# A planned instruction order made anew, with token maxima read from SBUF, in a kernel of soft mixture-of-experts, attention and gated layers

## The chip, the cores and the metric

The kernel runs on one core of one Trainium2 chip. The core has five engines with a queue each, worked off in order: PE (TensorE, the matrix multiplier), DVE (VectorE), ACT (ScalarE), POOL (GpSimd) and SP (SyncE, which here only issues DMAs). PE writes its results into PSUM; DVE and ACT read them there; POOL works on SBUF alone. The metric is the device time in microseconds of one execution, lower being better: the median of several runs. Everything is computed in float32.

## The reference, cut to what matters

The input `x` has 8 batches of 256 tokens of 128 features. Two groups of layers follow each other, and each sublayer adds to `x`:

```python
# soft mixture of experts: 16 experts of 64 slots, used in both groups
x1 = layernorm(x); se = layernorm(slot_embeds) * scale
logits   = einsum('bnd,esd->bnes', x1, se)
dispatch = softmax(logits, axis=1)                      # over the 256 tokens
combine  = softmax(logits.reshape(b, n, -1), axis=-1)   # over the 1024 slots
slots = einsum('bnd,bnes->besd', x1, dispatch)
eout  = (gelu(slots @ Wg + bg) * (slots @ Wu + bu)) @ Wd + bd
out   = einsum('bns,bso->bno', combine, eout)
# linear attention: elu + 1 features, 16 heads
# gated unit: gelu(gelu(silu(h w1) * (h w2) @ h1) @ h2) @ w3, ternary weights with scales
# random-feature attention (exp of projections, 16 heads of 32 features)
```

Each softmax needs maxima of the logits: `dispatch` one for each slot (over tokens), `combine` one for each token (over slots).

## The kernel before

**Steps and a planner.** The kernel doesn't issue its instructions where the Python text stands. Each piece of work is a *step* (`step`, L88): the engines that may do it with a planned length in ns each, the function that issues it, and the cells that it reads, writes and takes. `Plan.place` (L121) is a list scheduler. It takes the engines' clocks from 0 and repeatedly chooses among the steps that are ready the one that can start earliest (`rank = (at, s.key + 4 * late, s.number)`); a step's time `at` is the largest of its readiness (the end of what it needs, plus `LAG` of that engine), of its engine's free time, and of the time at which buffers of the kinds in `kinds` come free. Ties go to the smaller key. A key is the sum of planned PE time of the steps before it in the text, plus a shift of the step's part: the list `SHIFTS` (L16) has one number for each `plan.part()`, times 100. `TABLE` is the time for a change of ScalarE's function table. `Plan.issue` then writes the instructions in order of planned start. The plan is made when the kernel is built; on the chip each engine works through its queue in that order and waits on semaphores where it must.

**Lengths.** `act`, `dve`, `mms` and `flips` (L344 to L353) give planned lengths from a number of columns; other steps have a number written out.

**Norms.** `normalized` (L376) does a list of tiles of 128 x 128: per tile `bn_stats` and `bn_aggr` on DVE (L389, L390), then for all of them the *root* on POOL (L396 adds epsilon, L397 negates the mean, L398 raises to the power -0.5), then per tile one subtract and multiply (L404) on POOL or DVE, whichever the plan chooses. `norm` calls it for the two tiles of one batch.

**Dispatch of one batch** (`dispatch`, L547). The normalised tiles are flipped by PE (L359), copied with gain and bias by `affinely` (L446 on ACT, L448 on DVE), and spilled to DRAM and spread back in another layout by SP (L532, L539). Then come four pairs of logits matmuls (L568), each into one PSUM bank; each bank is copied to `comb` in SBUF (`evacuated`, L366 on ACT or L368 on DVE), and from the second on `greater` (L585, DVE) folds it into the token maxima `pm`. Its operands are the bank in PSUM and `comb` or `pm` in SBUF. After that, per half: `greatest` (L602, slot maxima, DVE), `exps` (L610, ACT), `inverse` (L618, DVE), `divided` (L623, POOL), a 32 x 32 block transpose (L631, DVE). PE gathers the slots (L644), and `affinely` writes them to `slots`. Last come the token maxima: `fold` (L661, DVE), two flips on PE, `token_max` (L672, DVE), two flips that spread them, a copy to `mb`; per half `less` (L690, POOL, subtracts them from `comb`) and an exponential (L696, ACT).

**The rest.** `experts` (L702) does 16 experts for four batches: L737 on PE, gelu L743 on ACT, L748 on DVE, L768 on PE. `combine` uses the exponentials of `comb` on PE (L809). Linear attention, gated units (`glu`; hidden products L1027) and random-feature attention follow. `group` (L1331 and on) runs this for four batches; the second group's keys are 45000 behind the first's. Layer 0 of a group calls `dispatch` for its four batches, then `experts`, then `combine` and the linear attention; layer 1 dispatches again. `weights` (L493) makes the block form of the projection weights (L504, DVE) once; `keys` (L453) normalises and flips the slot embeddings, two tiles at a time, into `seT`. Before all that PE multiplies the identity 14 times (`rehearse`).

Of the kernel before, what the change touches and what calls it, by code (L numbers as in the profile page):

```python
# [16 lines left out]
    -8021, -27496, -1880, -1692, -1246, -501, -3204, 428, -619, -9733, -3313, -704, -1426, -388,  # L17
    -970, -129, -74, -103, -98, -154, -167, -106, -115, -156, 74, -10, 102, 250, -97, -196,
    -808, -874, -909, -1074, 29, -1029, 38, -111, -648, 535, -462, -23, -50, -46, -16, -1, 45,
    -562, 6, 33, 30, -14, -15, 47, -634, -353, -62, -19, -6, 44, -80, -305, -75, -37, 23, -70,  # L20
    -46, -140, -62, -95, -51, -7, 41, 139, 595, 203, 505, 395, 466, 392, -421, -1494, -1666,
    -2400, -2447, -1620, -1321, -147, -1647, -2470, -682, -344, -440, -906, -1682, 131, 665,
    -678, -83, -257, -81, -105, -245, 128, -452, -242, 175, -164, 141, 89, -2895, 491, 27, -9,
    -309, 123, -400, -112, -68, -126, -154, -4, 30, -1, -18, -53, -63, -43, 40, -109, 28, -904,
    -346, -1059, -568, -335, 16, 114, 82, -63, 7, -540, -76, -46, 99, 125, 392, 168, 417, 581,
    1301, 1493, 564, -700, -58, 34, -703, -2087, -162, -669, 52, -105, 30, 443, -275, -282, 125,
    71, -25, 243, -231, -44, -662, -1357, -653, 10, 151, 122, 159, 89, 55, 401, -644, -846,
    -602, 288, 144, 168, 196, -340, 177, 49, -830, 47, 184, 1167, 295, 347, 468, 213, -1051,
    -596,
# [34 lines left out]
class Plan:  # L64
# [7 lines left out]
    LAG = {"PE": 300, "ACT": 120, "DVE": 100, "POOL": 150, "SP": 2600}  # L72
    TABLE = 1300
# [14 lines left out]
    def step(self, engines, run, reads=(), writes=(), takes=(), table=None):  # L88
        s = Step(len(self.steps), engines, run, table, self.key + self.shift)
        s.part = self.parts  # L90
        for c in reads:
            if c in self.writer:
                s.needs.add(self.writer[c])
        for c in writes:
            if c in self.writer:
                s.needs.add(self.writer[c])
            s.needs.update(self.readers.get(c, ()))
        for c in reads:
            self.readers.setdefault(c, set()).add(s)
        for c in writes:  # L100
            self.writer[c] = s
            self.readers[c] = set()
        s.needs.discard(s)
        for c in (*reads, *writes, *takes):
            b = c[0] if isinstance(c, tuple) else c
            if isinstance(b, Buf) and b not in s.bufs:
                s.bufs.append(b)
                b.left += 1
        self.steps.append(s)
        if "PE" in engines:  # L110
            self.key += engines["PE"]
        return s

    def given(self, at, cells):

        s = Step(-1, {}, None, None, 0)
        s.end, s.engine = at, "SP"
        for c in cells:
            self.writer[c] = s

    def place(self):  # L121
# [6 lines left out]
        free = dict.fromkeys(names, 0)  # L128
# [5 lines left out]
        def enable(s):  # L134
            s.ready = max((n.end + self.LAG[n.engine] for n in s.needs), default=0)
# [6 lines left out]
        while len(order) < len(self.steps):  # L142
            best = None
            for e in names:
                for s in able[e]:
                    at = max(s.ready, free[e])
                    short = {}
# [22 lines left out]
            if s.table:  # L170
                table = s.table
            for b in s.bufs:
# [6 lines left out]
            for b in s.bufs:  # L179
                b.left -= 1  # L180
                b.last = max(getattr(b, "last", 0), s.end + self.LAG[e])
# [19 lines left out]
def macaron_kernel(ctx: ExitStack, tc: tile.TileContext, i: dict, out: bass.AP):  # L201
# [65 lines left out]
    def fetched(dst, src, reads, writes):  # L267
        step({"SP": 430}, lambda _: nc.sync.dma_start(dst(), src), reads, writes)

    def x_in(b, n):  # L270
        fetched(
            lambda: x[:, b * TT : (b + n) * TT], i["x"][:, b * TT : (b + n) * TT],
            [], [("x", b + k) for k in range(n)],
# [70 lines left out]
    def act(n, pointers=False):  # L344
        return 160 + 0.83 * n + 100 * pointers

    def dve(n, extra=0):
        return 150 + 1.05 * n + extra

    def mms(*columns):  # L350
        return sum(2 * max(112, 0.84 * n) for n in columns)

    def flips(n):  # L353
        return 110 * n
# [21 lines left out]
    def normalized(tiles, twice=False):  # L376
# [9 lines left out]
        def stats(_):  # L386
            for t, (_, src, _, _) in enumerate(tiles):
                st = mv.ap[:, 8 + 6 * t : 14 + 6 * t]
                nc.vector.bn_stats(st, src())  # L389
# [10 lines left out]
        step({"DVE": 455 * n}, stats, [t[2] for t in tiles], [mv], takes=[t[3] for t in tiles])  # L400
        step({"POOL": 780 + 160 * n}, root, [mv], [mv])
        for t, (dst, src, r, w) in enumerate(tiles):
# [6 lines left out]
            step({"POOL": 480, "DVE": 430}, apply, [r, mv], [w])  # L409

    def norm(b, twice=False, y=None, at=0):

        y = y or Buf("k1", (P, TT, D))
        normalized(
            [
                (lambda t=t: y.ap[:, at + t, :], lambda t=t: x[:, b * TT + t, :],
                 ("x", b), (y, at + t))
# [4 lines left out]
        return y  # L422
# [18 lines left out]
    def affinely(dst, src, r, w, n):  # L441
# [8 lines left out]
        step({"ACT": act(n, True) + 90, "DVE": dve(n, 120)}, run, [*r, "ng"], w)  # L450


    def keys():  # L453
# [8 lines left out]
        for h in range(4):  # L462
            js = range(2 * h, 2 * h + 2)
            normalized(
                [
                    (lambda j=j: se_n.ap[:, j, :], lambda j=j: se_raw.ap[:, j, :],
                     (se_raw, h), (se_n, j))
                    for j in js
                ]
            )  # L470
# [22 lines left out]
    def weights():  # L493
# [24 lines left out]
        step({"POOL": 1900}, scaled, ["w3T", "s3"], ["w3T", "s3"])  # L518
# [7 lines left out]
    def replicated(y, b):  # L526
# [14 lines left out]
        step({"SP": 1800}, spill, [(y, t) for t in range(TT)], [("y", b)])  # L541
        step({"SP": 1800}, spread, [("y", b)], [yr])
# [4 lines left out]
    def dispatch(b, sl):  # L547
# [4 lines left out]
        y = norm(b, True)  # L552
# [10 lines left out]
        for u in range(4):  # L563
            pl = ps_(2, N)

            def logits(_, u=u, pl=pl):
# [10 lines left out]
                takes=[(comb, u), pm],  # L577
# [5 lines left out]
            if u:  # L583
                def greater(_, u=u, pl=pl):
                    nc.vector.tensor_tensor(  # L585
                        pm.ap, pl.ap, comb.ap[:, 0:2, :] if u == 1 else pm.ap, ALU.max
                    )

                step({"DVE": dve(2 * N)}, greater, [pl, pm, (comb, 0)], [pm])
# [6 lines left out]
        for h in range(2):  # L596
# [9 lines left out]
            step({"DVE": dve(4 * N)}, greatest, half, [mx])  # L606
# [8 lines left out]
            step({"ACT": 2200}, exps, [*half, mx], [mx, (ex, h)], table="exp")  # L615
# [4 lines left out]
            step({"DVE": 200}, inverse, [mx], [mx])  # L620
# [7 lines left out]
            step({"POOL": 1950}, divided, [mx, (ex, h)], [(ex, h)])  # L628
# [7 lines left out]
            step({"DVE": 1200}, turn, [(ex, h)], [(ex, h)])  # L636
# [12 lines left out]
        step({"PE": 3600}, gathered, [yr, (ex, 0), (ex, 1)], pos)  # L649
# [9 lines left out]

        def fold(_):  # L660
            nc.vector.tensor_tensor(pm.ap[:, 0], pm.ap[:, 0], pm.ap[:, 1], ALU.max)  # L661

        step({"DVE": 790}, fold, [pm], [pm])
# [21 lines left out]
        for h in range(2):  # L685
# [12 lines left out]
            step({"POOL": 2400}, less, [mb, *half], half)  # L698
# [3 lines left out]
    def experts(sl):  # L702
# [10 lines left out]
        def fetch(e):  # L713
# [11 lines left out]
            step({"SP": 1900}, run, [(sl, "in", BG - 2, 0)], [we])  # L725
            return we

        def front(e, we):
            j, k = e // 2, e % 2
            ht = Buf("k2", (P, 2, BG * S))  # L730
            for c in range(2):
# [25 lines left out]
                step({"DVE": dve(256, 65)}, up, [pe, ga], [(ht, c)])  # L757
            return ht

        def back(j, wes, hts):  # L760
# [3 lines left out]
            def down(_):  # L764
# [10 lines left out]
                {"PE": mms(*[P] * 2 * BG)}, down,  # L775
# [14 lines left out]
            step({"POOL": 120}, twos, [], whole(j))  # L790
# [11 lines left out]
    def combine(b, comb, sl, eo):  # L802
# [26 lines left out]
        step({"DVE": 900}, add, [(po, t) for t in range(TT)] + [("x", b)], [("x", b)], takes=[rc])  # L829

    def plus_bias(b, bias):
# [4 lines left out]
        step({"POOL": 750}, run, [("x", b)], [("x", b)])  # L836
# [30 lines left out]
    def linear(b):  # L867
        plan.part()
        yt = transposed(norm(b), TT)
# [37 lines left out]
        step({"ACT": act(512)}, exps, [kq], [kq], table="exp")  # L907
        step({"DVE": dve(512, 65)}, elu, [pk, kq], [kq])
# [5 lines left out]
        step({"POOL": 110}, ones, [pv], [(v1, 1)])  # L914
# [23 lines left out]
        step({"DVE": 730}, blocks, [pkv], [kv])  # L938
# [18 lines left out]
        step({"DVE": 1000}, divided, [po], [oh], takes=[rd])  # L957
# [5 lines left out]
    def combined_weights(name, scales, bufs, b):  # L963
# [12 lines left out]
        step({"SP": 2500}, fetch, [("x", b)], [*bufs, s])  # L976
# [9 lines left out]
        step({"POOL": 4 * 1050}, scaled, [*bufs, s], bufs)  # L986
# [8 lines left out]
        step({"POOL": 4 * 1200}, sums, bufs, bufs)  # L995
# [4 lines left out]
    def hidden(h, to, t4, w, wbufs):  # L1000
# [9 lines left out]
        def sub(dst, a, b, r, w):  # L1010
# [5 lines left out]
            step({"POOL": 1450, "DVE": 950}, run, r, w)  # L1016
# [30 lines left out]
        def gelu(i, k, src, r):  # L1047
# [3 lines left out]
            step({"ACT": act(512)}, run, r, [(to, i, k)], table="gelu")  # L1051
# [26 lines left out]
    def glu(b, after):  # L1078
# [8 lines left out]
        for k in range(2):  # L1087
            norm(b + k, False, y, k * TT)
# [3 lines left out]
        for o in range(NO):  # L1092
# [22 lines left out]
            step({"DVE": dve(512, 65)}, product, [pu, si], [(h, o // 2, k) for k in range(2)])  # L1115
# [27 lines left out]
    def favor(b):  # L1143
        plan.part()
        yt = transposed(norm(b), TT)
# [28 lines left out]
        step({"POOL": 1050}, squares, [(qk, 0)], [(qk, 1)])  # L1174
# [17 lines left out]
        step({"PE": 240}, half_norms, [(qk, 1)], [ph], takes=[hn])  # L1192
# [21 lines left out]
        for c, pw in enumerate(pws):  # L1214
# [13 lines left out]
            step({"DVE": 1550}, shifted, [pw, pn], [(phi, k, c) for k in range(2)], takes=[mx])  # L1228
        for k in (1, 0):
# [5 lines left out]
            step({"ACT": act(1024)}, exps, cells, cells, table="exp")  # L1235
# [49 lines left out]
        def turn_sums(_):  # L1285
# [4 lines left out]
            {"PE": 920}, sums, [*((phi, 1, c) for c in range(4)), v1], [pk], takes=[kv, kvm]  # L1290
        )
        step({"DVE": 430}, blocks, [pk], [kvm])
# [32 lines left out]
        step({"PE": 900}, products, [(qk, 0), (qk, 1), kv], [po], takes=[ot, rd])  # L1325
        step({"ACT": act(N), "DVE": dve(N)}, guarded, [po], [rd])
        step({"DVE": 2200}, divided, [po, rd], [ot])
# [3 lines left out]
    def group(g):  # L1331
        bs_ = range(g * BG, (g + 1) * BG)
        for layer in range(2):
            sl = Buf("slots", (P, NJ, 2, BG, S1))
            combs = {b: dispatch(b, sl) for b in bs_}
# [10 lines left out]
        def store(b):  # L1346
# [3 lines left out]
            step({"SP": 500}, run, [("x", b)], [])  # L1350
# [16 lines left out]
    step({"PE": 6000}, rehearse, [], [pwarm])  # L1367
# [76 lines left out]
```

## Time and profile before

| what | value |
|---|---|
| time, median of 3 runs | 762.42 us (761.95 to 763.28) |
| the profiled execution, its own time | 763.33 us |
| its span from first to last instruction | 761.6 us |
| busy: PE, DVE, ACT, POOL | 744.1, 527.4, 436.3, 321.2 us |
| matmuls of L737 (experts) | 512, 120.7 us |
| matmuls of L1027 (gated units), both forms | 896, 207.8 us |
| L585, token maxima, both forms, DVE | 48, mean 674 and 672 ns |
| L661, their fold, DVE | 16, mean 1056 ns |
| L404 on DVE; on POOL | 37, mean 644 ns; 59, mean 477 ns |
| L690 and L623 on POOL | 32 each, mean 2370 and 1906 ns |
| mean DMA over the span | 60 GB/s |

A PE matmul of float32 is two instructions in the profile. PE's time is its matmuls' time, with modelled ends; weight loads (PEld) run beside it. In the 40 slices of the page each digit is a tenth of a slice of 19.04 us, and PEclk is the granted clock, so the 8 in the first two slices means that PE ran below its full clock for a part of them.

### The profile page before, as it was taken

The page shows a single profiled execution, that of the slowest core. Times are in us where ns is not written, and L with a number is a line of the kernel's source. Part 1 is how long each engine was busy: PE and PEld are TensorE (multiplying, and loading weights), DVE is VectorE, ACT ScalarE, POOL GpSimd, SP SyncE. Part 2 cuts the span into 40 slices and gives each one's busy share as a digit, 9 for nine tenths or more (in the row PEclk, how much of TensorE's full clock was granted, in tenths as well). Part 3 has the DMA queues.
Part 4 walks back from the last instruction along what each step waited for, and adds up shares of the span by engine and source line. Part 5 has one row for each costly group of instructions (what it writes and reads, how often), then busy time and mean ns, then how long its engine had stood idle before and what let it go on. Part 6 is the DMA issues. An engine that isn't in the chain of part 4 may idle for free.

```text
span 761.6 us, 15125 instructions
## 1 busy us (share of the span) xinstructions
PE 744.1 (98%) x5884; PEld 623.3 (82%) x5884; DVE 527.4 (69%) x1085; ACT 436.3 (57%) x806; POOL 321.2 (42%) x418
## 2 busy tenths in 40 slices
PE   7889999999999999999999999999999999999998
PEld 6667788999889988889788987778867878878787
DVE  5898987467988787889645357756496737775432
ACT  2876988365676566791834245645265555493432
POOL 7766653442266652548901064334151622223020
PEclk8899999999999999999999999999999999999999
DMA  4634443113451043516322100000000000000000
GB/s 119 175 102 110 119 134 97 46 49 109 128 170 44 2 115 96 153 54 195 91 92 76 42 1 1 2 1 0 1 1 2 1 1 1 1 15 15 1 1 28
DMA packets 29911, 45.53 MB, mean 60 GB/s; under 512 B 5008, under 2 KB 18704, under 8 KB 29840
## 3 DMA queue, kind: packets, MB, share of 16 engines
q1 hardware_dynamic: 29840, 44.57, 19.7%
q8 instruction: 46, 0.75, 0.4%
q14 instruction: 25, 0.20, 0.1%
HBM read 41.41 MB, written 3.15 MB: 59 GB/s over the span
## 4 chain that ended last, share of the span: by engine, by line
PE 92%; DVE 4%; POOL 1%; issue 1%; ACT 1%; DMA 0%; DVEq 0%; POOLq 0%; ACTq 0%
PE ps L1027 26%; PE ps L737 14%; PE ps L768 8%; PE ps L809 8%; PE ps L644 7%; PE ps L568 6%; PE ps L359 4%; PE ps L1127 4%; PE ps L1100 4%; PE ps L1097 4%; PE ps L1206 1%; PE ps L1272 1%; PE ps L1306 1%; PE ps L857 1%; DVE comb L631 1%
## 5 line engine op out<-in xcount | busy, mean ns | idle before, releaser
L737 PE MATMUL ps<-slots,we 128*128 128x256 f32 x512 | 120.7, 385 | 0.4 <-DVE k L748 0.4
L737 PEld LDWEIGHTS ps<-slots,we 128*128 128x128 f32 x512 | 95.4, 192 | 14.9 <-issue 2.3
L1027 PE MATMUL ps<-comb,slots 128*128 128x256 f32 x448 | 104.0, 380 | 0.0
L1027 PE MATMUL ps<-comb,comb 128*128 128x256 f32 x448 | 103.8, 381 | 0.0
L1027 PEld LDWEIGHTS ps<-comb,slots 128*128 128x128 f32 x448 | 83.7, 190 | 15.3 <-issue 4.2
L1027 PEld LDWEIGHTS ps<-comb,comb 128*128 128x128 f32 x448 | 83.4, 190 | 13.0 <-issue 2.4
L690 POOL TENSOR_TENSOR comb<-comb,k 128x1024 f32<-128x1024 f32 x32 | 75.3, 2370 | 42.8 <-ACT k L366 32.0
L623 POOL TENSOR_TENSOR comb<-comb,sm 128x1024 f32<-128x1024 f32 x32 | 60.8, 1906 | 66.1 <-DVE sm L618 66.0
L366 ACT COPY k<-ps 128x512 f32<-128x512 f32 (+2 forms) x67 | 33.5, 503 | 86.9 <-PE ps L1027 61.9
L743 ACT ACTIVATE k<-ps,small 128x256 f32<-128x256 f32 x128 | 57.4, 474 | 42.5 <-PE ps L737 40.4
L748 DVE SCALAR_TENSOR_TENSOR k<-ps,small,k 128x256 f32<-128x256 f32 x128 | 56.9, 475 | 22.7 <-ACT k L743 22.3
L644 PE MATMUL ps<-comb,k 32*128 32x256 f32 x1024 | 65.1, 393 | 3.2 <-issue 1.3
L610 ACT ACTIVATE comb<-comb,sm 128x256 f32<-128x256 f32 x128 | 63.2, 496 | 7.6 <-DVE sm L602 7.5
L568 PE MATMUL ps<-k,seT 128*128 128x256 f32 x256 | 63.5, 394 | 1.7 <-ACT k L446 0.9
L644 PEld LDWEIGHTS ps<-comb,k 32*128 32x128 f32 x1024 | 54.8, 192 | 10.4 <-issue 3.0
L1049 ACT ACTIVATE comb<-comb 128x512 f32<-128x512 f32 x48 | 29.9, 629 | 58.0 <-DVE comb L1041 57.8
L768 PEld LDWEIGHTS ps<-we,k 128*64 128x64 f32 x1024 | 55.3, 137 | 9.4 <-issue 5.0
L768 PE MATMUL ps<-we,k 128*64 128x128 f32 x1024 | 62.5, 276 | 0.0
L1041 DVE TENSOR_TENSOR comb<-ps,k 128x512 f32<-128x512 f32 x48 | 32.9, 687 | 40.7 <-PE ps L1027 31.4
L809 PE MATMUL ps<-slots,comb 128*128 128x129 f32 x512 | 60.0, 276 | 0.0
L809 PEld LDWEIGHTS ps<-slots,comb 128*128 128x128 f32 x512 | 58.6, 192 | 1.3 <-issue 1.2
L1012 POOL TENSOR_TENSOR comb<-comb 128x512 f32<-128x512 f32 x18 | 27.3, 1519 | 75.9 <-DVE comb L1106 47.5
(147 smaller groups left out, 1354.0 us busy)
## 6 DMA issues: line engine op xcount, KB each, us to landing
we<-in_We SPq DMA_DIRECT2D x64, 384.0 KB, 3.9
k<-y SPq DMA_DIRECT2D x64, 128.0 KB, 2.8
y<-k SPq DMA_DIRECT2D x64, 32.0 KB, 1.9
we<-in_bd SPq DMA_DIRECT2D x64, 32.0 KB, 3.6
comb<-in_h2T SPq DMA_DIRECT2D x4, 256.0 KB, 3.6
slots<-in_h1T SPq DMA_DIRECT2D x4, 256.0 KB, 3.4
out<-x SPq DMA_DIRECT2D x8, 128.0 KB, 1.7
x<-in_x SPq DMA_DIRECT2D x3, 256.0 KB, 4.8
```

The costliest lines, as they stand in the source:

```text
L366: nc.scalar.copy(dst(), src())
L568: mm(pl.ap[:, j, :], seT[:, 2 * u + j].rearrange("p k s -> p (k s)"), yt.ap, start=True, stop=True,)
L610: nc.scalar.activation(ex.ap[:, 4 * h + j, :], comb.ap[:, 4 * h + j, :], AF.Exp, bias=mx.ap[:, j : j + 1], accum_out=mx.ap[:, 4 + j : 5 + j],)
L623: nc.gpsimd.tensor_tensor(ex.ap[:, part], ex.ap[:, part], mx.ap[:, 8:12].unsqueeze(2).to_broadcast([P, 4, N]), ALU.mult,)
L644: mm(po.ap, yr.ap[rows, c, :], ex.ap[rows, :, 32 * c : 32 * c + 32], start=(c == 0), stop=(c == N // 32 - 1), tile_position=(32 * a, 0),)
L690: nc.gpsimd.tensor_tensor(raw, raw, mb.ap.unsqueeze(1).to_broadcast([P, 4, N]), ALU.subtract)
L737: mm(pe.ap[:, m, :], we.ap[:, ts(2 * m + c, P)], sl.ap[:, j, k, :, 0:S], start=True, stop=True,)
L743: nc.scalar.activation(ga.ap, pe.ap[:, 0, :], AF.Gelu, bias=bg[:, e, c : c + 1])
L748: nc.vector.scalar_tensor_tensor(ht.ap[:, c, :], pe.ap[:, 1, :], bu[:, e, c : c + 1], ga.ap, ALU.add, ALU.mult,)
L768: mm(po.ap[S * k : S * k + S, q, :], hts[k].ap[:, c, ts(q, S)], wes[k].ap[:, ts(4 + c, P)], start=(c == 0), stop=(c == 1), tile_position=( ...
L809: mm(po.ap[:, t, 0 : D + 1], comb.ap[:, j, ts(t, P)], eo()[:, j, q, 0 : D + 1], start=(j == 0), stop=(j == NJ - 1),)
L1027: mm(bank.ap[:, o], w(k)[:, c, ts(o, P)], rhs().rearrange("p (c n) -> p c n", c=2)[:, c, :], start=(start and o + c == 0), stop=(stop and ...
```

## The change

Four things are done together.

1. **The planner.** A step can have a flag `port`: on DVE it uses the way to SBUF that DVE and POOL share. Such a step on DVE isn't planned before POOL is free, and no POOL step is planned before it ends. A step can have its own `lag` beside its engine's. Engines start at 800 instead of 0. Lags, the table time and nearly all lengths have new numbers, DMA steps (spill, spread, weight fetches, loads) among them.
2. **Token maxima.** The three `greater` steps of a batch move from between the logits to the third part of `dispatch`, behind the gathering matmuls. They read `comb` in SBUF instead of the PSUM bank. They, the fold, the subtract-and-multiply of norms and the subtractions L1012 of the gated units have `port=True`.
3. **Roots of four tiles.** `norm` takes a list of batches, and statistics are steps of two tiles each under one root. Keys have two roots of four tiles; in the first layer the batches from the third on are normalised in pairs; each gated unit has one root for its two batches.
4. **Order.** `SHIFTS` is another list of numbers.

The diff, cut to its core:

```diff
-    -8021, -27496, -1880, -1692, -1246, -501, -3204, 428, -619, -9733, -3313, -704, -1426, -388,
...
+    -12747, -60125, 1443, -759, -665, 112, -292, -428, -5344, 35, -525, -35, -44, 180, -46, -44,
...
-    LAG = {"PE": 300, "ACT": 120, "DVE": 100, "POOL": 150, "SP": 2600}
-    TABLE = 1300
+    LAG = {"PE": 205, "ACT": 170, "DVE": 150, "POOL": 130, "SP": 2000}
+    TABLE = 1295
...
+                    if e == "POOL":
+                        at = max(at, port)
+                    elif e == "DVE" and s.port:
+                        at = max(at, free["POOL"])
...
+            if e == "DVE" and s.port:
+                port = s.end
...
     def act(n, pointers=False):
-        return 160 + 0.83 * n + 100 * pointers
+        return 48 + 0.871 * n + 87 * pointers
     def dve(n, extra=0):
-        return 150 + 1.05 * n + extra
+        return 58 + 1.07 * n + extra
...
-        step({"DVE": 455 * n}, stats, [t[2] for t in tiles], [mv], takes=[t[3] for t in tiles])
-        step({"POOL": 780 + 160 * n}, root, [mv], [mv])
+        for t in range(0, n, 2):
+            step(
+                {"DVE": 810}, lambda e, t=t: stats(e, (t, t + 1)), [z[2] for z in tiles[t : t + 2]],
+                [(mv, t)], takes=[z[3] for z in tiles[t : t + 2]],
+            )
+        step({"POOL": 765 + 160 * n}, root, [(mv, t) for t in range(0, n, 2)], [mv])
...
-            step({"POOL": 480, "DVE": 430}, apply, [r, mv], [w])
+            step({"POOL": 432, "DVE": 262}, apply, [r, mv], [w], port=True)
...
-        step({"SP": 1800}, spill, [(y, t) for t in range(TT)], [("y", b)])
-        step({"SP": 1800}, spread, [("y", b)], [yr])
+        step({"SP": 2500}, spill, [(y, t) for t in range(TT)], [("y", b)], lag=-1500)
+        step({"SP": 1765}, spread, [("y", b)], [yr], lag=900)
...
-        y = norm(b, True)
+        if not first or b < 2:
+            (y,) = norm([b], True)
+        else:
+            if b % 2 == 0:
+                normed[:] = norm([b, b + 1], True)
+            y = normed[b % 2]
...
-            if u:
-                def greater(_, u=u, pl=pl):
-                    nc.vector.tensor_tensor(
-                        pm.ap, pl.ap, comb.ap[:, 0:2, :] if u == 1 else pm.ap, ALU.max
-                    )
-
-                step({"DVE": dve(2 * N)}, greater, [pl, pm, (comb, 0)], [pm])
...
+        for u in range(1, 4):
+            def greater(_, u=u):
+                nc.vector.tensor_tensor(
+                    pm.ap, comb.ap[:, 2 * u : 2 * u + 2, :],
+                    comb.ap[:, 0:2, :] if u == 1 else pm.ap, ALU.max,
+                )
+
+            step(
+                {"DVE": dve(2 * N)}, greater, [(comb, u), (comb, 0)] if u == 1 else [(comb, u)],
+                [pm], port=True,
+            )
...
-        step({"DVE": 790}, fold, [pm], [pm])
+        step({"DVE": 330}, fold, [pm], [pm], port=True)
...
-            step({"POOL": 1450, "DVE": 950}, run, r, w)
+            step({"POOL": 1380, "DVE": 608}, run, r, w, port=True)
```

## The prediction

> **What bounds the kernel now.** I read first the two clocks of the page: the busy rows and the granted clock in 40 slices of 19 us each.
>
> ```profile
> span 761.6 us, 15125 instructions
> PE   7889999999999999999999999999999999999998
> DVE  5898987467988787889645357756496737775432
> POOL 7766653442266652548901064334151622223020
> PEclk8899999999999999999999999999999999999999
> ```
>
> TensorE is nearly never idle after the fourth slice; before it, it idles a little and runs twice below its full clock. VectorE is at eight to nine tenths there. Then I cut the span into stretches at the points where the granted clock changes (columns: stretch, its length, busy time of PE, PE's weight load, VectorE, ScalarE, GpSimd, granted clock, DMA share, GB/s).
>
> ```profile
> 0.00:11.00 11.00, 7.80 (x35) 6.87 (x36) 6.08 (x29) 2.31 (x4) 7.19 (x30) 1.00 0.52 147
> 11.00:17.90 6.90, 6.17 (x17) 4.67 (x17) 4.17 (x18) 2.40 (x5) 5.64 (x16) 0.51 0.21 56
> 17.90:31.50 13.60, 10.33 (x51) 8.17 (x49) 12.36 (x18) 12.27 (x40) 9.29 (x8) 1.00 0.68 192
> 31.50:38.30 6.80, 6.80 (x56) 4.91 (x58) 5.08 (x8) 4.92 (x15) 5.35 (x3) 0.50 0.59 153
> 38.30:62.20 23.90, 18.81 (x236) 15.77 (x229) 22.72 (x47) 15.25 (x41) 16.79 (x19) 1.00 0.27 83
> 62.20:65.70 3.50, 3.50 (x12) 2.74 (x11) 0.24 (x2) 2.61 (x4) 2.52 (x6) 0.51 0.18 46
> 65.70:160.00 94.30, 93.11 (x858) 81.03 (x856) 72.82 (x140) 74.84 (x149) 44.93 (x38) 1.00 0.34 100
> ```
>
> Up to 62.2 us PE's busy times sum to 49.9, so it idles 12.3 us. In the three stretches at half clock it is busy 6.17 + 6.80 + 3.50 = 16.5 us, of which half, 8.2 us, is the price of the clock. From 65.7 to 160 it idles 1.2 us, and in the stretches 160 to 360 and 360 to the end another 0.9 and 3.1 us. So about 20 us can be won ahead of 65.7, and 5 behind it: the kernel is bound by PE, but its beginning by what feeds PE. What feeds it, the chain of waits tells (start, length, what):
>
> ```profile
> 30.52 0.59 DVE k L585
> 31.15 7.80 PE ps L644 x60
> ...
> 42.12 1.31 DVE k L661
> 43.43 2.25 DVE sm L602 x2
> 45.69 0.33 DVE sm L672
> ...
> 53.45 2.39 DVE pbd L504
> 55.84 0.34 DVE k L661
> ```
>
> VectorE's own queue stands on the chain, and among its steps are those that the change moves: the token maxima (L585), their fold (L661) and their reduction (L672), which nothing needs before the combination, whose first matmul (L809) is at 136 us.
>
> **Part by part, against the profiled execution (763.33 us, span 761.6).**
>
> *Maxima late in order.* The chain ahead of 62 us holds L585 four times (0.59 + 3 x 0.58 = 2.33), L661 twice (1.31 + 0.34) and L672 twice (0.38 at 25.46, and 0.33): 4.7 us. All 48 L585 lose their PSUM source; the fold and the reduction follow them; then come PE's two flips each, GpSimd's subtraction L690 (two of 2.37 us a batch) and ScalarE's exponentials, which move with them. GpSimd is 42% busy and waits 42.8 us ahead of L690 as it is; for the first batches these have some 100 us of slack. The logits' PSUM banks come free after the copy alone, some 0.67 us sooner, which PE (waiting for no bank in the chain) doesn't need now. VectorE gets the moved work back behind 65.7, where it is busy 72.8 of 94.3 us: 21 us are free there, for 12 L585 of 0.67 and 4 folds and reductions, 11 us. If that cover fails, it is the first rival's case. But "late" is only a key that breaks ties among steps that can start at once: the hand-set shifts give the maxima of the first three batches smaller keys (a hundred times -665, -428 and -525, beside their place) than the fourth batch's softmax (-44), so I expect about a third, 1.6 us, to stay on the chain. **Net 3.1.**
>
> *The way to SBUF that two engines share.* Here row and rule bear against the change. Now L585 reads one operand from PSUM; its 48 instructions never stretch. The fold reads both from SBUF:
>
> ```profile
> L661 DVE TENSOR_TENSOR k<-k x16: 391/748/2462, 22.1 to 357.2; 128x256 f32<-128x256 f32 x16
> L585 DVE TENSOR_TENSOR k<-ps,k x32: 652/679/691, 18.8 to 356.1; 128x512 f32<-128x512 f32 x32
> L585 DVE TENSOR_TENSOR k<-ps,comb x16: 651/678/691, 17.1 to 328.6; 128x512 f32<-128x512 f32 x16
> ```
>
> Shortest, median and longest in ns: the fold needs 391 alone and up to 2462 where a GpSimd operation holds the way. The Trainium skill (SBUF — State Buffer, Who interferes with whom) says of this that a VectorE instruction with two SBUF inputs and a GpSimd instruction that reads SBUF exclude each other for the whole instruction, whichever came first. The change turns 48 instructions into that form. By the rule, met at random, with GpSimd busy 0.7 of the time ahead of 62 us in operations of about 2.1 us, each waits 0.7 x 1.05 = 0.7 us more (an estimate): 12 of them are 9 us on VectorE's queue there, and the change would lose. By the row the same form at this size (L1012, two SBUF inputs) has a mean of 1175 and a minimum of 675: 0.5 more each. Against that stands the new rule of the plan: such a step starts only when GpSimd is free, and another VectorE step goes first. I take the cost of a maximum met well, 0.69 against 0.67, plus one in four met badly: 12 x 0.5 / 4 = 1.5 us, of which a third lies on the chain: **minus 0.5** (bounds: 0, and minus 6 for 12 x 0.5 all on the chain).
>
> *L504*, the block of projection weights, is such a form too (0.4 or less by the fold's 391 for a larger one, but 2.39 behind a GpSimd operation at 53.45). It isn't marked for the shared way, so its luck is open: between 0 and 2.0 gained, **1.0**. L404 on VectorE (median 346, longest 2365) is marked now; its stretches sum to 37 x (644 - 346) = 11 us over the whole span, nearly all beside a full PE: nothing.
>
> *Roots of four tiles.* A root is three GpSimd instructions, 209 + 193 + 698 = 1.10 us for two tiles. Keys need two instead of four, six batches of the first layer's dispatch three instead of six, each of eight gated units one instead of two. No row has four columns; the bounds for one are 1.1 (a fixed price) and 1.4 (the plan's 160 ns a tile more). GpSimd saves 0.8 to 1.1 us per pair, but the first half of a four waits for the statistics of two tiles more, 0.9 us on VectorE (0.271 + 0.182 each). At the beginning the second tile of the first batch is normalised only at 10.31 and the first logits start at 12.27, while its root ended at 5.7: a better order can start them near 10. That PE then runs at half clock takes back half. **1.0** (bounds 0 and 2.0). For the units PE is full: nothing.
>
> *The clock.* The half-clock stretches at 31.50 and 62.20 follow 3.4 us in which PE was busy 1.05 and 1.96 us (28.10 to 31.50 and 58.80 to 62.20). The Trainium skill (TensorE: Matmul & The Clock Gate, Part 1) lets the clock halve after an idle window of about 3.4 us; here a thin one was enough, so the trace decides. By the rule alone a shorter gap would be forgiven, and both stretches' 3.4 + 1.75 us come back; by the trace a gap only a little shorter still halves it. Bounds 0 and 5.1; nearer to the trace: **1.0**.
>
> *Plan's lengths, lags, table time, first free time, DMA lags.* They add no instruction and no DMA; they move steps past each other on all queues: spills and spreads to and from DRAM (5.38 us of issue for two batches' eight, planned at 1.8 each before and 2.5 now), expert weights, stores. One thing that a truer plan can mend: PE's order puts the flips of the second group's tiles (61.65) ahead of the first expert's matmul (61.97), though the last slots were written by 60.3: 1.6 us, of which I count a quarter, **0.4**. Behind 65.7 an order can win at most 5 us and lose more: nothing.
>
> Sum: 3.1 - 0.5 + 1.0 + 1.0 + 1.0 + 0.4 = 6.0 us; 763.33 - 6.0 = 757.3. The median of the runs shown is 0.9 below the profiled one, so **756.4 us**.
>
> **Rivals.**
> *The late maxima come due in front of PE (slower).* PE works in a fixed order. Where its flips of the maxima are placed ahead of other work and the fold is held up by GpSimd, all behind them waits: at 43.49 and 46.17 the trace has this, 0.53 us (behind L661) and 2.24 us (behind L672), 2.8 in all. Each batch and layer has one such pair, 16; with the maxima later there is less slack to the subtraction and the combination. From three such stalls on (8.4 us) the 6.0 are gone; with four, one at each of the four changes from experts to combination, and one thin window that halves the clock for 6.8 us (3.4), it is 756.4 + 11.2 + 3.4 = 771; with four and no halving 767.6. For it: 48 instructions of a worse form, and tighter lags (PE's from 300 to 205 ns). Against: after 65.7 PE waited for the maxima 1.7 us in all, and has other batches' work. I take 767.
>
> *The beginning really opens up (faster).* VectorE is busy 50.4 us up to 62.2; the 12 L585 (8.1), the folds (2.7), the reductions (1.6) all leave it and the experts start near 52 us, with both later half-clock stretches gone: 763.3 - 0.9 - 12 = 750.4. For it: 22.72 of 23.90 us busy. Against: the keys, and that softmax work runs in a row over four engines.
>
> *Nothing moves (same).* The order of the beginning stays set by the softmax chain itself (L602, L610, L623, L631), and each wait that goes uncovers the next: 762.4. The cover for it: in 17.90 to 31.50 ScalarE is busy 12.27 of 13.60 too.
>
> **How the numbers follow.** A measurement of this kernel can tell about 0.2%, 1.5 us, from no change. Forecast (2 to 9 us gained) 0.49, the open beginning 0.18, no change 0.09, late maxima or another bad wait in the new order 0.24. Faster 0.67, same 0.09, slower 0.24. The likeliest case alone runs from 753 to 760; since its rival on the other side has a quarter, the range runs from 749 (most of the open beginning) to 767 (four stalls).
>
> **What would show it.** Right: no maxima on the chain before the first L737, this one before 57 us; L585's successor with a median near 0.7; first logits near 10 us; PE idle below 9 us ahead of the experts. Wrong: PE idle over 2 us behind the maxima's flips after 100 us; a fourth half-clock stretch; maxima with a mean over 1.1 us on VectorE ahead of the experts; or experts' start unmoved at 62 us.

## The result, and the profile after

| | before | changed |
|---|---|---|
| median of 20 runs each | 761.30 us (759.89 to 763.78) | 760.07 us (757.59 to 763.84) |
| ratio of the changed to before | | 0.9981, 95% interval 0.9969 to 0.9992 |
| span of the profiled execution | 761.6 us | 758.9 us |

The change makes the kernel 0.19% faster, 1.4 us of the 6.0 that were forecast. The page of the changed kernel (busy tenths in 40 slices, and the granted clock):

```profile
span 758.9 us, 15049 instructions
PE   7897999999999999999999999999999999999998
DVE  7975887478988789974663555463878787856342
POOL 7965294343626444660660210122435332210000
PEclk9998999999999999999999999999999999999999
```

The first three slices, 57 us, now run at full clock. In the fourth the PE digit falls to 7 and the clock to 8. The span, cut where this kernel's clock and waits change, shows where (stretch, length, busy PE, PE's weight load, VectorE, ScalarE, GpSimd, clock, DMA share, GB/s):

```profile
38.00:56.60 18.60, 18.55 (x229) 16.75 (x230) 15.07 (x23) 16.08 (x43) 12.21 (x7) 1.00 0.57 158
56.60:63.20 6.60, 1.88 (x9) 1.32 (x7) 0.78 (x4) 6.51 (x8) 3.64 (x3) 1.00 0.88 204
63.20:70.00 6.80, 6.15 (x15) 4.43 (x16) 4.56 (x9) 1.22 (x3) 1.57 (x1) 0.50 0.00 0
```

From 56.6 to 63.2 us PE is busy 1.88 us of 6.60 and VectorE 0.78; for the next 6.8 us the clock is halved. PE's timeline (start, length, what, idle time before it and who ended it; the first line is of the kernel before) shows the experts begin at 56.59 us, 5.2 us sooner than before, and stop after one expert's matmuls:

```profile
61.81 3.21 PE L737 MATMUL ps<-slots,we 128*128 128x256 f32 x8
...
56.59 1.89 PE L765 MATMUL ps<-slots,we 128*128 128x256 f32 x8
63.74 2.07 PE L765 MATMUL ps<-slots,we 128*128 128x256 f32 x4 [5.26 <-DVE slots L460]
```

The chain of waits (start, length, what) tells why VectorE was late with the slots (L460):

```profile
30.20 2.33 DVE k L675
...
58.81 3.51 DMA projT<-in_projT
...
62.42 0.29 DVE pbd L517
62.71 0.09 DVE sm L631
62.80 0.88 DVE slots L460 x2
```

L517 is the block form of the projection weights, L504 of the kernel before. It stands in VectorE's queue ahead of the slots and waits for projT to land, although nobody needs its result until the random-feature attention (first matmul with it at 532.4 us). In the order before, SP issued projT at 25.50 us; now it stands behind spills, spreads and expert weights, as SP's timelines show (first line before, the others changed):

```profile
25.50 0.33 SPq L268 DMA_DIRECT2D projT<-in_projT  x1
...
52.38 5.74 SPq L552 DMA_DIRECT2D k<-y  x8
58.17 0.42 SPq L275 DMA_DIRECT2D bo<-in_bo  x1
58.81 0.35 SPq L275 DMA_DIRECT2D projT<-in_projT  x1
```

VectorE therefore does nothing for 9.35 us, with the slots' copies waiting behind the block:

```profile
62.42 0.29 DVE L517 TENSOR_TENSOR pbd<-projT,m4of 128x128 f32<-128x128 f32 x1 [9.35 <-DMA projT<-in_projT]
```

To compare runs by stretch I made an estimate: I took, from the traces, the end of each matmul and set against every stretch the time that its matmuls need back to back at full clock (216 ns an instruction for 256 columns, 112 for 128, 430 for 512, 57 for the row-tiled gathering, and so on, the same for every kernel: 718.6 us in all). What is left is PE's *lost time*, idle or slow clock, in us; it is the differences between kernels that count:

| kernel | 0-60 | 60-100 | 100-400 | 400 to the last matmul | sum |
|---|---|---|---|---|---|
| before | 22.4 | 5.3 | 7.0 | 5.2 | 39.9 |
| changed | 12.6 | 8.6 | 11.5 | 4.4 | 37.1 |

So the beginning won 9.8 us, more than was forecast; 3.3 of it went in the stretch of the projT wait, and 4.5 between 100 and 400 us. Each row is one profiled execution. That of the kernel before took 763.33 us, 2.0 more than the median of 20, and that of the changed one 760.57, 0.5 more; so the rows differ by 2.8 us where the medians differ by 1.2.

### The profile page after: what moved, and what is told of

Its sections match the earlier page's. It is cut to its first block, busy times and chain, and to the rows that moved or that the text cites. A ratio compares the mean times of both kernels' runs of the same rounds, so it can differ in the third digit from the quotient of the medians.

```text
span 758.9 us, 15049 instructions
## 1 busy us (share of the span) xinstructions
PE 735.9 (97%) x5884; PEld 616.9 (81%) x5884; DVE 521.1 (69%) x1096; ACT 447.0 (59%) x823; POOL 287.5 (38%) x360
## 4 chain that ended last, share of the span: by engine, by line
PE 86%; DVE 6%; DMA 4%; SPq 2%; POOL 1%; issue 1%; ACT 0%; POOLq 0%; DVEq 0%
PE ps L1055 26%; PE ps L765 13%; PE ps L796 7%; PE ps L837 7%; PE ps L657 6%; PE ps L1154 4%; PE ps L366 4%; PE ps L1124 4%; PE ps L1127 4%; PE ps L588 4%; DMA we<-in_We 2%; DVE sm L615 1%; PE ps L1233 1%; PE ps L1299 1%; PE ps L1333 1%; PE ps L885 1%
## 5 line engine op out<-in xcount | busy, mean ns | idle before, releaser
L765 PE MATMUL ps<-slots,we 128*128 128x256 f32 x512 | 122.6, 388 | 8.1 <-DVE slots L460 5.3
L636 POOL TENSOR_TENSOR comb<-comb,sm 128x1024 f32<-128x1024 f32 x32 | 62.9, 1971 | 72.1 <-DVE sm L631 68.3
L771 ACT ACTIVATE k<-ps,small 128x256 f32<-128x256 f32 x128 | 55.6, 475 | 36.1 <-PE ps L765 32.5
L588 PE MATMUL ps<-k,seT 128*128 128x256 f32 x256 | 61.6, 383 | 2.2 <-ACT k L458 1.3
L403 POOL TENSOR_SCALAR sm<-sm 128x2 f32<-128x2 f32 (+1 forms) x39 | 7.9, 203 | 143.7 <-DVE sm L397 142.4
L796 PEld LDWEIGHTS ps<-we,k 128*64 128x64 f32 x1024 | 55.4, 137 | 8.3 <-issue 3.2
L796 PE MATMUL ps<-we,k 128*64 128x128 f32 x1024 | 61.6, 275 | 0.0
L657 PE MATMUL ps<-comb,k 32*128 32x256 f32 x1024 | 59.8, 380 | 1.0 <-DVE comb L644 1.0
L657 PEld LDWEIGHTS ps<-comb,k 32*128 32x128 f32 x1024 | 52.2, 185 | 6.0 <-issue 2.0
```

Of the source, the lines that this page charges most:

```text
L588: mm(pl.ap[:, j, :], seT[:, 2 * u + j].rearrange("p k s -> p (k s)"), yt.ap, start=True, stop=True,)
L636: nc.gpsimd.tensor_tensor(ex.ap[:, part], ex.ap[:, part], mx.ap[:, 8:12].unsqueeze(2).to_broadcast([P, 4, N]), ALU.mult,)
L657: mm(po.ap, yr.ap[rows, c, :], ex.ap[rows, :, 32 * c : 32 * c + 32], start=(c == 0), stop=(c == N // 32 - 1), tile_position=(32 * a, 0),)
L765: mm(pe.ap[:, m, :], we.ap[:, ts(2 * m + c, P)], sl.ap[:, j, k, :, 0:S], start=True, stop=True,)
L771: nc.scalar.activation(ga.ap, pe.ap[:, 0, :], AF.Gelu, bias=bg[:, e, c : c + 1])
L796: mm(po.ap[S * k : S * k + S, q, :], hts[k].ap[:, c, ts(q, S)], wes[k].ap[:, ts(4 + c, P)], start=(c == 0), stop=(c == 1), tile_position=( ...
```

## The experiments

Six of the eight experiments keep a plan: the order is made as it was, and then only what the diff names is moved or altered, so nothing else is meant to change place in any queue. Numbers 5 and 6 let the planner make a new order.

**1. The block issued later.** In the changed kernel:

```diff
-        step({"DVE": 500}, block, ["projT"], ["pbd"])
+        step({"DVE": 500}, block, ["projT"], ["pbd"]).late = 60000
...
-        for s in sorted(self.placed, key=lambda s: (s.start, s.number)):
+        for s in sorted(self.placed, key=lambda s: (s.start + s.late, s.number)):
```

> The changed kernel, its whole plan kept, with one VectorE step (the block form of projT, L517) issued far later in VectorE's queue. Theory 1 (VectorE's queue stood 9.35 us behind this step for a DMA, PE 5.26 us behind the slots, and the clock was halved for 6.8 us after it): both go, 5.3 + about 3 us; 751 to 755 us, no half-clock stretch near 63 us, PE's wait for L460 below 1 us, VectorE's idle time ahead of 70 us near 9 us less. Theory 2 (the wait uncovers the next one: spreads or expert weights on SP's queue, which issues without a gap to 61 us): PE still idles 4 us or more between 56 and 70 us; 758 to 761 us.

Measured: 755.47 us, ratio to before 0.9929 (0.9914 to 0.9944). PE's timeline:

```profile
57.79 2.75 PE L766 MATMUL ps<-slots,we 128*128 128x256 f32 x12
60.38 0.38 PE L367 MATMUL ps<-ident,k 128*128 128x128 f32 x2
60.60 1.89 PE L766 MATMUL ps<-slots,we 128*128 128x256 f32 x8
64.56 0.43 PE L367 MATMUL ps<-ident,sm 128*128 128x128 f32 x2 [2.07 <-DVE sm L698]
```

The wait for the slots is gone, and so is the half clock at 63 us. Theory 1 holds for place and for sign; the size fell 0.5 us short of its range, since part of Theory 2 came true at once: PE's flips of a batch's maxima now wait 2.07 us for the reduction L698. In front of that reduction stand two maxima, beside two of GpSimd's divisions:

```profile
59.25 4.37 POOL L637 TENSOR_TENSOR comb<-comb,sm 128x1024 f32<-128x1024 f32 x2
59.49 4.68 DVE L676 TENSOR_TENSOR k<-comb 128x512 f32<-128x512 f32 x2
```

They took 2.38 us each, where the median is 0.68: the plan keeps such steps apart from GpSimd, the chip's times did not. PE's lost time between 60 and 100 us falls from 8.6 to 4.6.

**2. projT loaded early.** The changed kernel, with the two loads given the planned start of WoT's:

```diff
+        first = next(s for s in self.steps if s.mark == "WoT")
+        for s in self.steps:
+            if s.mark in ("bo", "projT"):
+                s.start = first.start
```

> The changed kernel, its plan kept, with the loads of bo and projT issued right behind WoT (near 19 us) instead of at 58 us. Theory 1: as with the late block, 751 to 755 us, with L517 begun before 54 us. Theory 2: 758 to 761 us. If SP's queue itself is what is late, two more issues (0.9 us) ahead of the spills cost up to 0.9 us against the late block.

Measured: 755.02 us, ratio 0.9936 (0.9914 to 0.9959), not told apart from experiment 1. SP issued projT at 19.28 us and the block began at 53.07, without a wait:

```profile
19.28 0.33 SPq L280 DMA_DIRECT2D projT<-in_projT  x1
...
53.07 0.47 DVE L523 TENSOR_TENSOR pbd<-projT,m4of 128x128 f32<-128x128 f32 x1
```

Two opposite edits, one of VectorE's queue and one of SP's, both remove the same loss: its cause is the block waiting for this load. A wait of 2.10 us for the reduction of the maxima is left here too, with 3.4 us at half clock behind it, from 63.8 us.

**3. The same block late in the kernel before.** The diff of experiment 1, on the kernel before.

> The kernel before, its plan kept, with the same block step (L504, 2.39 us on the chain) issued far later. The prediction's step took 1.0 us for it between 0 and 2.0. Theory 1 (it is on the chain and nothing lies beside it): 1 to 2.4 us faster than before. Theory 2 (POOL's roots and PE's order of flips take its place at once): no change, within 0.5 us.

Measured: 760.56 us, ratio 0.9999 (0.9991 to 1.0008). Theory 2 in size: the 2.39 us that L504 had on the chain were worth nothing. Not in what it named: no root of GpSimd is on the chain there. It runs through the slot gathering on PE (5.44 and 7.25 us), with 3.4 us at half clock from 48.1 us in place of those at 62.2, and the first expert starts at 61.28 instead of 61.81 us.

**4. Maxima from SBUF in the order before.** The kernel before, its plan kept; the maxima change their operand, and each is issued where it stood or right behind the copy of its bank:

```diff
-                        pm.ap, pl.ap, comb.ap[:, 0:2, :] if u == 1 else pm.ap, ALU.max
+                        pm.ap, comb.ap[:, 2 * u : 2 * u + 2, :],
+                        comb.ap[:, 0:2, :] if u == 1 else pm.ap, ALU.max,
...
```

> The kernel before, its plan and its order kept, but the 48 token maxima (L585) read comb in SBUF instead of the PSUM bank, each where it stood or right behind the copy of its bank. This is the price of the form alone, met by a plan that doesn't know of the shared way. By the rule (0.7 us more each ahead of 62 us) 6 us slower or more; by the row of L1012 (0.5 more each, 12 of them on or near the chain, all on the chain) up to 6 slower; the prediction's own view (a third of 12 x 0.5 on the chain) 2 us slower; if VectorE's queue has slack there, no change. Mean of one near 1.1 us.

Measured: 772.14 us, ratio 1.0152 (1.0133 to 1.0172): 11.3 us slower. Its groups of instructions (busy us, mean ns | idle before):

```profile
L595 DVE TENSOR_TENSOR k<-comb,k 128x512 f32<-128x512 f32 x32 | 36.2, 1135 | 1.1 <-ACT comb L374 1.0
L595 DVE TENSOR_TENSOR k<-comb 128x512 f32<-128x512 f32 x16 | 18.0, 1128 | 2.4 <-ACT comb L374 1.9
```

and PE's longest waits (total us, times, longest):

```profile
PE ps L367 <- DVE k L674: 7.2, 4, 5.5
PE ps L577 <- ACT k L454: 4.2, 2, 3.3
PE ps L367 <- DVE sm L685: 2.6, 2, 2.0
```

A maximum takes 1.13 us on average instead of 0.67, the experts start at 67.1 us instead of 61.8, and PE waits for the fold (L674) and the reduction (L685). In the traces VectorE's 1085 instructions have the same order in both kernels, and it waits for bank copies ahead of the maxima as long as before (1.0 and 1.9 us), so it is the form that costs. In a plan that doesn't know of the way to SBUF, it costs more than the 6 us that the prediction had set as a bound. The changed kernel's own maxima, by contrast (shortest, median, longest in ns):

```profile
L675 DVE TENSOR_TENSOR k<-comb,k x32: 643/681/2410, 30.1 to 330.2; 128x512 f32<-128x512 f32 x32
L675 DVE TENSOR_TENSOR k<-comb x16: 649/682/711, 24.2 to 314.2; 128x512 f32<-128x512 f32 x16
L686 DVE TENSOR_TENSOR k<-k x16: 383/416/2117, 44.8 to 330.9; 128x256 f32<-128x256 f32 x16
```

Their mean is (27.9 + 10.8) / 48 = 0.81 us, and the fold's median fell from 748 to 416. Four of the 48 took 1.9 to 2.4 us, against 17 over 1 us in experiment 4. So the two engines meet less often in the new order; how much of that is the flag and how much the later place, no run separates.

**5. Maxima alone, planned anew.** The kernel before with the maxima's code of the change and all else old, so the old planner makes a new order from the old shifts.

> The kernel before with the token maxima moved and read from SBUF, nothing else: old planner, old lengths, old shifts, so the order is planned anew without tuning. The prediction's sum for this part: 3.1 - 0.5 = 2.6 us faster. The rule of the shared way, met at random by a plan that doesn't know of it: L585's successor with a mean of 1.1 us or more, up to 6 us slower. An untuned order alone may cost several us more; then PE idles behind 66 us where it didn't.

Measured: 804.88 us, ratio 1.0576 (1.0561 to 1.0590). Their mean is (37.3 + 15.4) / 48 = 1.10 us. But most of PE's lost time isn't near them (0-60: 27.5; 100-400: 33.5 us), so a control was needed.

**6. The control: the kernel before, planned anew.** A memset's planned length is 65 instead of 120, nothing else.

> The kernel before with one planned length changed (a memset of 106 ns, planned with 65 instead of 120), so that the old shifts meet a planner that decides otherwise somewhere; the work is the same. It is the control for the maxima alone (804.9 us). If an untuned order is what cost 44 us there, this one loses many us too (over 5). If the maxima's form and place cost it, this one is within 2 us of before.

Measured: 784.14 us, ratio 1.0310 (1.0290 to 1.0329). The same work in an order that nobody tuned costs 23 us, 26.8 us of lost time lying between 100 and 400. Experiment 5 can't be read as the price of the maxima; experiment 4 can, since it keeps the order.

**7. Roots of two tiles again.** Experiment 1's kernel, its plan kept, with

```diff
-            nc.gpsimd.tensor_tensor(v, v, power[:, 0:n], ALU.pow)
+                nc.gpsimd.tensor_tensor(v, v, power[:, 0:2], ALU.pow)
```

and the two instructions before it likewise, in a loop over pairs of tiles.

> The changed kernel with the late block (755.5 us), its plan kept, with each root of four tiles issued as two roots of two. GpSimd works 0.7 to 1.1 us more at each of the 13 roots of four. The prediction took 1.0 us for the roots, between 0 and 2.0: 755.5 to 757.5 us, first logits 0.7 to 1.5 us later. If the roots give nothing, 755.5.

Measured: 756.56 us, ratio 0.9945 (0.9927 to 0.9963), against 0.9929 (0.9914 to 0.9944) with roots of four: the medians differ by 1.1 us, the intervals overlap. GpSimd's power in experiment 1 and here (start, length, what):

```profile
7.24 1.01 POOL L406 TENSOR_TENSOR sm<-sm,power 128x4 f32<-128x4 f32 x1
```

```profile
7.22 0.69 POOL L407 TENSOR_TENSOR sm<-sm,power 128x2 f32<-128x2 f32 x1
```

A power of four columns costs 0.32 us more than one of two, as the plan assumed. The first logits start at 11.03 instead of 10.40 us. The forecast's 1.0 us is in keeping with this, not proved by it. By lost time (table below) the splitting costs 2.6 us ahead of 60 us, and 2.1 come back between 100 and 400, in one execution each.

**8. The clock held up in the kernel before.** Its plan kept, with 18 matmuls of the identity ahead of the first gathering, into a bank that is overwritten afterwards:

```diff
+            if not filled:
+                filled.append(1)
+                for _ in range(18):
+                    mm(pos[0].ap[:, 0:4, :], ident, ident, start=True, stop=True)
```

> The kernel before, its plan kept, with 18 matmuls of the identity (about 2 us of PE at full clock) ahead of the first gathering, where PE waits from 28.1 to 31.2 us; their result is overwritten. If the thin window of 28.1 to 31.5 us is what halves the clock for the next 6.8 us, that stretch goes and 60 gathering matmuls of 7.8 us take 3.9 less: 2 to 3.5 us faster, unless the gathering's successors wait for VectorE anyway (then no change). If the fill only delays the gathering, up to 2 us slower.

Measured: 760.72 us, ratio 0.9995 (0.9987 to 1.0003): no change. PE's timeline:

```profile
27.26 4.18 PE L644 MATMUL ps<-ident 128*128 128x128 f32 x36
31.37 0.71 PE L648 MATMUL ps<-comb,k 32*128 32x256 f32 x6
32.23 3.72 PE L648 MATMUL ps<-comb,k 32*128 32x256 f32 x58 [0.15 <-DVE k L585]
35.87 3.72 PE L568 MATMUL ps<-k,seT 128*128 128x256 f32 x16
41.84 0.44 PE L359 MATMUL ps<-ident,k 128*128 128x128 f32 x2 [2.25 <-DVE k L665]
44.52 0.66 PE L359 MATMUL ps<-ident,sm 128*128 128x128 f32 x2 [2.24 <-DVE sm L676]
```

The fill does keep the clock here: the stretch at half clock from 31.5 us is gone, and 58 gathering matmuls take 3.72 us where 60 had taken 7.80. Then PE waits 2.25 us for the fold, where it had waited 0.53. The first expert is 1.3 us earlier, and even that doesn't reach the median. But a half-clock stretch as long starts at 43.6 us, behind that wait (columns as in the stretches above):

```profile
43.60:50.40 6.80, 5.48 (x46) 5.11 (x50) 5.91 (x10) 3.40 (x14) 4.74 (x3) 0.50 0.36 110
```

In all, half clock falls only from 17.0 to 13.6 us. So the run shows that the slow clock at 31.5 us wasn't what set the time, since VectorE was behind it; it doesn't show that slow clock is free. Executions of one kernel even speak against that. Of the 19 of the kernel before that were timed beside experiments 4, 6, 7 and 8, five had a mean granted clock of 0.987 and took 762.12 to 762.47 us, and five had 0.991 and took 759.77 to 760.59. Slow clock and time go together there, about 2 us for some 6 us at half clock (an estimate: 0.004 of 761 us, twice); which of the two causes the other isn't shown.

PE's lost time in three of the runs that keep a plan:

| kernel | 0-60 | 60-100 | 100-400 | 400 to the last matmul | sum |
|---|---|---|---|---|---|
| block late, changed | 12.2 | 4.6 | 10.6 | 4.6 | 32.0 |
| roots of two, block late, changed | 14.8 | 4.3 | 8.5 | 4.7 | 32.3 |
| SBUF maxima in the order before | 27.3 | 5.8 | 10.1 | 5.6 | 48.8 |

**Still open.** What costs the changed orders 1.5 to 4.5 us more than before between 100 and 400 us is seen, not tried. PE's longest waits in that stretch (total us, times, longest), before and then changed:

```profile
PE ps L359 <- DVE k L661: 0.9, 1, 0.9
PE ps L359 <- DVE sm L672: 0.5, 1, 0.5
```

```profile
PE ps L765 <- DMA we<-in_We: 2.0, 4, 1.0
PE ps L366 <- DVE k L415: 1.8, 2, 0.9
PE ps L366 <- DVE k L686: 1.1, 1, 1.1
PE ps L366 <- ACT slots L458: 1.1, 1, 1.1
```

They sum to 1.4 and 6.0 us, about the 4.5 that were lost: four waits for expert weights, two for normalised tiles, one for the fold of late maxima, one for slots. SP's issues of expert weights wait for L796 (before L768), the second matmuls with such weights, in both kernels (99.3 and 86.2 us in this stretch); only in the new order does PE come to wait for the weights. The new planner without its flag for the shared way, and the maxima in their old place under the new shifts, weren't tried.

## Why the prediction was wrong

The sign was right; the size was a quarter of the forecast. By its own steps:

- **L504, "between 0 and 2.0 gained, 1.0".** This is the step that failed. I priced only its bad luck with GpSimd and let it end at 0 on the losing side, without following the load that it waits for. The new order put that load from 25.5 to 58.8 us in SP's queue, the block then held VectorE 9.35 us, and PE 5.26 us with a halved clock behind. Undoing it brings 4.6 us in medians of different sessions, 0.52% or 4.0 us by the ratios (0.9981 to 0.9929): the term was about -4, not +1.0. And as a gain it was nothing (experiment 3).
- **The sum without it.** With the block moved the ratio is 0.9929, and the forecast, 756.4 from 762.4, is 0.992. That this agrees is in part luck: by the lost time, 10.2 us were won ahead of 60 us, where 6.0 were forecast, and 3.6 were lost between 100 and 400, where nothing was.
- **"Plan's lengths, lags ...: they add no instruction and no DMA", 0.4, and behind 65.7 nothing.** Loads of constants such as projT were not among the moved DMAs that I named. Between 100 and 400 us the new order lost 4.5 us; I had said that it can lose more than it wins, and then counted nothing.
- **Maxima late, net 3.1, with a third left on the chain.** L675 was still there ahead of the experts (0.06 and 2.33 us, half of the 4.7 and not a third), so "no maxima on the chain" was wrong. The experts' start before 57 us was right (56.59), and so was PE's idle time ahead of them, 56.6 - 49.1 = 7.5 us, below 9. How much of the 9.8 us ahead of 60 us belongs to the lateness, and how much to the rest of the order, no run separates.
- **The shared way, minus 0.5, a maximum at 0.69 with one in four met badly.** That is 0.69 + 0.5 / 4 = 0.82 us, and 0.81 was measured, by luck: one in twelve was met badly, at three times the price (four maxima, 1.2 to 1.7 us more each). My estimate by the rule of the Trainium skill (SBUF — State Buffer, Who interferes with whom), 0.7 us more for each maximum ahead of 62 us, was right for a plan that doesn't know of it: in experiment 4 the twelve ahead of the experts took 1.42 us on average against 0.67, so 0.75 more. Over all 48 it was 0.46 more (1.13), and the kernel lost 11.3 us, about half of 48 x 0.46 = 22. My bound of 6 held for the beginning, where PE's lost time rose by 4.9 us; it put the other 36 maxima at nothing, and they cost 4.0 us more by the same measure.
- **Roots, 1.0.** First logits at 10.36 us against "near 10"; the splitting costs 1.1 us in medians (experiment 7), within the noise.
- **The clock, 1.0 with bounds 0 and 5.1.** All three half-clock stretches up to 66 us are absent from the changed profile, and a new one of 6.8 us came with the projT wait. What the clock alone is worth stays open: speeding up the stretch at 31.5 us gave nothing (experiment 8), so its 3.4 us of slow clock and the wait behind it were in part the same loss, and my sum of some 20 us to be won counted both.
- **Rivals.** Late maxima stood in front of PE once in the changed kernel, with 1.13 us at 101.3 us, and twice in experiment 1 (2.07 and 1.12 us), where the projT wait no longer covered the first; from three stalls of 2.8 us on they would have decided. The open beginning came nearly true (9.8 us by PE's lost time ahead of 60 us) and 7.8 us of it were given back between 60 and 400 us.

The version of experiment 1 or 2, one step moved by hand, beats both kernels: 755.5 and 755.0 us.

## What to carry to other kernels

When an order is made anew, look in each in-order queue for steps whose result isn't needed soon but whose input comes by DMA, and follow that input through the issuing queue: one such step can hold everything behind it. A hand-tuned order is part of the kernel's time (23 us here for a change of one planned length), so test a part of a change with the order kept, and run a control where it can't be kept. Slow-clock time and idle time of an engine that waits for another can be the same loss seen twice; don't add them without a test.

## What the runs showed of the hardware that wasn't expected

VectorE's maxima with two SBUF operands, met at random by GpSimd, took 1.13 us against 0.67 for 512 columns, and half of that stretching reached the end of the kernel, although VectorE is busy only 69% of the span. In the new order, planned to keep the two apart, it was 0.81 us, but the plan does not exclude a meeting: with one other step moved, two maxima took 2.38 us each beside GpSimd again (experiment 1). PE's clock was halved after 3.4 us with 1.05 us of matmuls in them. With 18 matmuls of no use put in, it stayed full there and was halved for as long 12 us later; the kernel's time stayed the same.
